# Planning fill work around pairs of Gelu blocks in a four-layer attention kernel

## The chip, the cores and the metric

The kernel runs on one core of a Trainium2 chip. The core has a matrix engine (TensorE, called PE in the profile; its weight loads are PEld), a vector engine (VectorE, DVE), a scalar engine for activation functions (ScalarE, ACT), a general engine (GpSimd, POOL) and an engine that here issues DMA transfers (SyncE, SP). Each engine runs its own instructions in order, and semaphores keep them in step. The metric is the device time of one execution in microseconds (us).

## The reference, cut to what matters

Four attention layers run one after the other on x of shape (4, 1024, 256), with a context of 77 rows, 16 heads of width 16. Only the first two layers, called L0 and L1, are touched by the change, and of them the feed-forward part of L0 above all:

```python
qkv = (_ln(x, g1, be1) @ w_qkv + b_qkv)             # L0, heads of 16
k = concat([k_self, k_ctx]); v = concat([v_self, v_ctx])
scores = einsum('bthd,bshd->bhts', q, k) * scale    # 1024 x 1101, causal
attn = softmax(where(mask, scores, -inf))
x = x + einsum('bhts,bshd->bthd', attn, v)
hdn = _ln(_ln(x, g2, be2), gf, bf) @ w1 + b1        # 256 -> 1024
hdn = gelu(hdn, approximate=False)
x = x + (hdn @ w2 + b2)                             # 1024 -> 256
# L1: rmsnorm; a linear attention over Taylor features of the context
#     plus a causal window of 64; both concatenated @ Wout, added to x
# L2: cross attention with weights and a mask, layer norm
# L3: rmsnorm, cross attention, added to x -> output
```

All of it is in 32-bit floats.

## The kernel before, in words

**Steps.** L0 and L1 are worked off in steps, one for each batch `b` (4) and each group of four heads (`quad`, 4), so 16 steps for each layer. A step computes two things side by side: the row maxima of the scores of its own unit, and the exponentials and weighted sums (weights) of the unit before it. Items of both kinds are paired (`pair_up`); in a full L0 step there are 11 maxima items (`Max0`) and 12 weight items (`Sum0`), in an L1 step four `Max1` and six of `Lin1` and `Win1`.

**Bursts and gaps.** For a pair, `step` issues two bursts of score matmuls. Each burst fills two PSUM tiles `ps` (`pair_tile`, pool `big`, two buffers, line 40): one half is for the maxima and is read by VectorE (lines 644 and 651, in L1 line 1113), the other is for the weights and is read by an Exp on ScalarE (line 716, in L1 lines 1151 and 1189). An item without a partner gets a burst in which both tiles have the same reader. Since there are two buffers and a burst takes both, the next burst's matmuls wait until ScalarE and VectorE have read this one. The time between is a gap, in which PE does other work: behind the second burst of a pair the weighted sums of the item before (matmuls pv, pvw or pvl from pe), and then fill.

**Fill.** Fill is the work of other stages that runs along: projections (pp, ppv) of the next unit, products of the context for the later layers, and the feed-forward part of an earlier batch (`ffn`, line 856). Each is a Python generator that issues one piece at each `next`, wrapped in a `Job` (line 440) with its number of pieces in this step, the share of the step over which they are to be spread (`a` to `b`) and, for work on PE, the planned time of one piece, `us`. The functions `jobs0` and `jobs1` list the jobs of each step. `gap` runs the pieces without a planned time up to the present share (layer norms, transposes, statistics, on VectorE, GpSimd and PE); `fill` runs pieces with a planned time, always of the job that is most late, until the planned time of the gap is used.

**The plan of a step.** `step` estimates for each burst how long PE must be kept busy in the gap behind it (`reads`), from the columns `c` that its readers read and the columns `f` of the sums that stand in the gap anyway. Then it raises or lowers all of them by one level until they add up to the fill work of this step (`needs`):

```python
reads = [0.3 + n * (0.1 + c / 455.0) - f / 600.0 for *_, n, c, f in bursts]
...
needs = [max(0.0, r + lo) for r in reads]
```

What a gap uses too much or too little is carried to the next (`left`; `put` counts the issued matmul columns / 600). The share of the step that is passed to `gap` and `fill` is the sum of the needs so far by their total.

**The feed-forward part.** `ffn` of one batch is 64 pieces of 0.85 planned us. The 1024 rows are cut into four blocks. For each block eight pieces compute ph (256 columns, two matmuls each), with the bias added by VectorE into a tile hT (line 874). With the eighth, ScalarE runs two Gelus in place, over two hT tiles of 128 x 1024 (line 880). So a pair of Gelus is issued with the pieces 8, 24, 40 and 56. Between them stand the pieces of the second product (po from w and hT) of the block before, of which every second one or more issues nothing. The 64 pieces are spread over four steps: 15, 11, 24 and 14 of them for the batches 0 and 1 (from the step (1, 2), by batch and quad, on), 15, 11, 22 and 16 for batch 2, and 17, 12, 17 and 18 for batch 3. So 16 steps hold ffn work, ten of L0 and six of L1.

ScalarE needs a table load (ACT_TABLE_LOAD) when it changes from Exp to Gelu and another on the way back.

Of the kernel before, what the change touches and what calls it, by code (L numbers as in the profile page):

```python
# [31 lines left out]
def tile_xattn_seq(ctx: ExitStack, tc: tile.TileContext, d: dict, out: bass.AP):  # L32
# [6 lines left out]
    work = first.enter_context(tc.tile_pool(name="work", bufs=2))  # L39
# [4 lines left out]
    put = [0.0]  # L44
# [395 lines left out]
    class Job:  # L440

        def __init__(self, gen, n, a=0.0, b=1.0, rest=False, us=0.0):
            self.gen, self.n, self.a, self.b, self.did, self.rest = gen, n, a, b, 0, rest
            self.us = us

        def late(self, share):

            want = self.n * min(1.0, max(0.0, (share - self.a) / (self.b - self.a)))  # L450
            return want - self.did
# [46 lines left out]
    def burst(parts):  # L498

        rows = [it.matmuls(p, ps) for it, p, ps in parts]  # L500
        for i in range(max(len(r) for r in rows)):
            for r in rows:
                if i < len(r):
                    for args, kw in r[i]:
                        mm(*args, skip_group_check=True, **kw)
        for it, p, ps in parts:
            it.take(p, ps)

    def pair_tile():
        return big.tile([P, 2, 512], F32, name="ps", tag="big")  # L510

    def step(items, jobs):

        bursts = []
        behind = 0
        for m, t in items:
            cols = max(i.cols for i in (m, t) if i)
            if m and t:  # L520
                for p in range(2):
                    bursts.append(((m, p), (t, 1 - p), p and t, 1, cols, p * behind))
            else:
                one = m or t
                bursts.append(((one, 0), (one, 1), t, 2, cols, behind if t else 0))
            if t:
                behind = t.cols
        work = sum(j.n * j.us for j in jobs)
        if work:
            reads = [0.3 + n * (0.1 + c / 455.0) - f / 600.0 for *_, n, c, f in bursts]  # L530

            lo, hi = -3.0, 30.0
            for _ in range(40):
                more = (lo + hi) / 2
                if sum(max(0.0, r + more) for r in reads) > work:
                    hi = more
                else:
                    lo = more
            needs = [max(0.0, r + lo) for r in reads]
        else:  # L540
            needs = [max(160.0, 140 + n * c - 0.8 * f) for *_, n, c, f in bursts]
        total, at, left = sum(needs), 0.0, 0.0
        for (*parts, t, _, _, _), need in zip(bursts, needs):
            burst([(i, p, pair_tile()) for i, p in parts])
            if t and pending:
                pending.pop(0)()
            at += need
            left += need
            was = put[0]
            gap(at / total, jobs)  # L550
            fill(at / total, jobs, was + left)
            left -= put[0] - was
            if t:
                pending.append(t.sums)
        for j in jobs:
            j.end()
# [1055 lines left out]
    def keep(key, gen):  # L1612
        if key not in live:
            live[key] = gen()
        return live[key]

    def jobs0(b, quad):

        j = []
        if quad % 2 == 0:  # L1620
            a = 0.4 if (b, quad) == (0, 0) else 0.0
            j.append(Job(keep(("h0", b, quad // 2), None), 1, a, a + 0.01, True))
        if (b, quad) in ((0, 0), (0, 2), (1, 0)):
            more_places()
        if b == 0 and quad == 0:
            j.append(Job(later_constants(), 3, 0.0, 0.4))
            j.append(Job(keep("c00", None), 1, 0.1, 0.2, us=0.85))
            j.append(Job(values0(0, 0), 4, 0.2, 0.8, us=0.85))
            j.append(Job(other_contexts(), 3, 0.0, 0.1))
            j.append(Job(feature_weights(), 3, 0.5, 1.0))  # L1630
            j.append(Job(values2(), 5, 0.3, 0.9, us=0.85))
            j.append(Job(keys2(), 4, 0.5, 0.9, us=0.5))
        if (b, quad) == (0, 1):
            j.append(Job(heads3("wk"), 8, 0.0, 1.0, us=1.03))
        if (b, quad) == (0, 2):
            j.append(Job(keys3(), 16, 0.0, 1.0, us=1.03))
        if (b, quad) == (0, 3):
            j.append(Job(heads3("wv"), 8, 0.0, 1.0, us=1.03))
        if (b, quad) in ((1, 0), (1, 1)):
            j.append(Job(keep("f3", folded3), 15 - 6 * quad, 0.0, 1.0, quad == 1, us=0.85))  # L1640
        if quad == 0 and b + 1 < NB:
            j.append(Job(stats0(b + 1), 8, 0.3 if b == 0 else 0.0, 1.0))
        if quad == 1:
            j.append(Job(values0(b, 1), 4, 0.15, 0.95, us=0.85))
            j.append(Job(keep(("h0", b, 1), lambda: heads0(b, 1, units)), 4, 0.0, 0.85, us=1.7))
            if b:
                j.append(Job(ffn_norms(b - 1), 24, 0.2, 1.0))
        if quad == 2:
            if b:
                j.append(Job(ffn_features(b - 1), 8, 0.0, 0.35))  # L1650
            if b + 1 < NB:
                j.append(Job(features0(b + 1), 8, 0.62, 1.0))
            else:
                j.append(Job(stats1(0), 8, 0.0, 0.5))
                j.append(Job(features1(0), 8, 0.62, 1.0))
        if quad == 3:
            if b + 1 < NB:
                j.append(Job(values0(b + 1, 0), 4, 0.15, 0.9, us=0.85))
                j.append(Job(context0(b + 1), 2, 0.0, 0.4, us=0.9))
                j.append(Job(keep(("h0", b + 1, 0), lambda: heads0(b + 1, 0, units)), 4, 0.15, 0.85, us=1.7))  # L1660
            else:
                j.append(Job(context1(0), 3, 0.3, 0.5))
                j.append(Job(values1(0, 0), 4, 0.4, 0.95, us=0.85))
                j.append(Job(keep(("h1", 0, 0), lambda: heads1(0, 0, units)), 4, 0.45, 0.85, us=1.7))
        for fb, n, a, last in (
            (b - 1, 15, 0.4, 0) if quad == 2 else (b - 1, 11, 0.0, 0) if quad == 3 else
            (b - 2, 24, 0.0, 0) if quad == 0 else (b - 2, 14, 0.0, 1),
        ):
            if fb >= 0:
                j.append(Job(keep(("ffn", fb), lambda: ffn(fb)), n, a, 0.97, last, us=0.85))  # L1670
        return j

    def jobs1(b, quad):
        j = []
        h = 4 * b + quad
        if h <= 1:
            j.append(Job(keep(("ffn", 2), None), (22, 16)[h], 0.0, 1.0, h == 1, us=0.85))
        if h == 1:
            j.append(Job(ffn_norms(3), 24, 0.2, 1.0))
        if h == 2:  # L1680
            j.append(Job(ffn_features(3), 8, 0.0, 0.3))
        if 2 <= h <= 5:
            j.append(Job(keep(("ffn", 3), lambda: ffn(3)), (17, 12, 17, 18)[h - 2],
                         0.35 if h == 2 else 0.0, 1.0, h == 5, us=0.85))
        if quad % 2 == 0:

            j.append(Job(keep(("h1", b, quad // 2), None), 1, 0.0, 0.01, True))
        if quad < 2:

            j.append(Job(keep(("h1", b, 1), lambda: heads1(b, 1, units)), 2,  # L1690
                         0.0 if quad else 0.2, 0.75 if quad else 0.95, us=1.7))
        if quad == 1:
            j.append(Job(values1(b, 1), 4, 0.15, 0.95, us=0.85))
        if b + 1 < NB:
            if quad == 1:
                j.append(Job(stats1(b + 1), 8, 0.0, 0.8))
            if quad == 2:
                j.append(Job(features1(b + 1), 8, *((0.35, 0.65) if h == 2 else (0.0, 0.5))))
            if quad == 3:
                j.append(Job(context1(b + 1), 3, 0.0, 0.3, us=0.85))  # L1700
                j.append(Job(values1(b + 1, 0), 4, 0.2, 0.95, us=0.85))
            if quad > 1:
                j.append(Job(keep(("h1", b + 1, 0), lambda: heads1(b + 1, 0, units)), 2,
                             0.0 if quad == 3 else 0.7 if h == 2 else 0.55, 0.75 if quad == 3 else 1.0, us=1.7))
        cb, half, n, a, last = (
            (b - 1, 0, 8, 0.0, 1), (b - 1, 1, 4, 0.4, 0), (b - 1, 1, 8, 0.0, 1), (b, 0, 4, 0.4, 0)
        )[quad]
        if cb >= 0:
            j.append(Job(keep(("comb", cb, half), lambda: combine1(cb, half)), n, a, 1.0, last, us=0.75))
        return j  # L1710
# [136 lines left out]
```

## Time and profile before

| | us |
|---|---|
| median of three runs | 2319.71 (2314.33 to 2328.15) |
| the profiled execution | 2315.78 |
| its span, first to last instruction | 2314.1 |
| TensorE busy | 2143.2 |
| VectorE busy | 1512.5 |
| ScalarE busy | 1027.2 |
| GpSimd busy | 642.6 |
| first and last Gelu pair, start of its table load | 445.0 and 1363.4 |
| one Exp over two heads (128 x 1024) | 1.024 |
| one Gelu (128 x 1024) | 1.050 |
| one table load | 1.283 |

The steps with ffn work lie between about 436 and 1400 us of the span. A line of a timeline reads: start in us, duration, engine, line, operation, tile written <- tiles read, shape, number of instructions merged; in brackets the idle time of the engine before it and what ended that. A line of groups ends with the busy time in us, the mean ns of one instruction, and the idle time before them with what ended it. A line of windows has the window, its length, the busy time of PE, PEld, DVE, ACT and POOL with the number of instructions, the granted TensorE clock (1.00 is full), the DMA share and GB/s. Matmuls overlap in the pipeline, so the durations of a merged group are a little longer than the distance to the next group.

### The profile page before, as it was taken

How to read it: one execution, taken by the hardware profiler on the slowest of the kernel's cores; microseconds unless marked ns; L12 is line 12 of the kernel's file. 1: busy time of each engine (PE TensorE's matmuls, PEld its weight loads, DVE VectorE, ACT ScalarE, POOL GpSimd, SP SyncE). 2: the span in 40 equal slices, each digit the busy share in tenths (PEclk: the TensorE clock that was granted, in tenths of full speed). 3: DMA queues.
4: the chain of work that ended last, by engine and by line, in shares of the span. 5: the costliest groups of instructions: out<-in, count | busy, mean ns of one | idle time of the engine just before them, and what ended most of it. 6: DMA issues, size and time to landing. Idle time of an engine off the chain costs nothing.

```text
span 2314.1 us, 41236 instructions
## 1 busy us (share of the span) xinstructions
PE 2143.2 (93%) x16842; PEld 1356.8 (59%) x16874; DVE 1512.5 (65%) x2492; ACT 1027.2 (44%) x1700; POOL 642.6 (28%) x927
## 2 busy tenths in 40 slices
PE   4999998999999999999989999999889998899999
PEld 2444444455555555455456666656556777788887
DVE  3756567755576545755386567777759999677664
ACT  1244444434444444344433444444448876432222
POOL 2011113011131112310152233333323655542221
PEclk9999999999999999999999999999999999999999
DMA  7221121100000000101010010101023334102200
GB/s 218 55 66 57 43 57 38 40 6 15 5 17 2 10 11 6 38 1 19 3 18 6 15 31 15 21 17 19 15 77 123 115 108 127 47 15 58 58 14 17
DMA packets 87858, 93.98 MB, mean 41 GB/s; under 512 B 35714, under 2 KB 77558, under 8 KB 87542
## 3 DMA queue, kind: packets, MB, share of 16 engines
q1 hardware_dynamic: 87670, 91.35, 15.0%
q8 instruction: 133, 2.18, 0.4%
q14 instruction: 55, 0.45, 0.1%
HBM read 55.31 MB, written 18.39 MB: 32 GB/s over the span
## 4 chain that ended last, share of the span: by engine, by line
PE 66%; DVE 16%; ACT 5%; issue 2%; POOL 1%; DMA 0%; ACTq 0%; SPq 0%; DVEq 0%; POOLq 0%
PE ps L51 27%; PE po L51 13%; PE pp L51 5%; DVE mpart L651 4%; PE ph L51 4%; PE pv L51 4%; DVE ms L1113 3%; PE psT L1350 2%; PE pvT L51 2%; PE ppv L51 2%; DVE mrow L1117 1%; PE pm L570 1%; ACT pe L716 1%; PE ptx L339 1%; PE pvw L51 1%
## 5 line engine op out<-in xcount | busy, mean ns | idle before, releaser
L51 PE MATMUL ps<-qk 32*128 32x192 f32 (+8 forms) x6528 | 589.5, 425 | 72.9 <-DVE mpart L651 32.0
L716 ACT ACTIVATE pe<-ps 128x1024 f32<-128x1024 f32 (+2 forms) x384 | 363.3, 952 | 581.5 <-PE ps L51 574.2
L51 PEld LDWEIGHTS ps<-qk 32*128 32x128 f32 (+1 forms) x6528 | 316.9, 183 | 335.4 <-DVE mpart L651 96.8
L651 DVE TENSOR_REDUCE mpart<-ps 128x2 f32<-128x1024 f32 (+4 forms) x384 | 331.1, 885 | 233.4 <-PE ps L51 232.7
L719 POOL TENSOR_SCALAR_AFFINE_SELECT pe<-pe 128x256 f32<-128x256 f32 (+1 forms) x192 | 94.9, 495 | 672.6 <-ACT pe L716 671.8
L1189 ACT ACTIVATE pew<-ps 128x768 f32<-128x768 f32 x128 | 103.4, 811 | 165.9 <-PE ps L51 165.6
L1351 ACT COPY pT<-psT 128x512 f32<-128x512 f32 (+1 forms) x192 | 92.3, 518 | 175.4 <-PE psT L1350 174.9
L1194 POOL TENSOR_SCALAR_AFFINE_SELECT pew<-pew 128x512 f32<-128x512 f32 x128 | 81.7, 638 | 302.2 <-ACT pew L1189 302.2
L51 PE MATMUL pv<-pe,va 128*32 128x512 f32 (+3 forms) x1536 | 157.1, 496 | 0.0
L1113 DVE TENSOR_TENSOR ms<-ps,maskw 128x768 f32<-128x768 f32 x128 | 122.1, 954 | 45.6 <-PE ps L51 42.7
L51 PE MATMUL po<-U,pT 128*128 128x256 f32 (+1 forms) x640 | 143.7, 380 | 0.2
L51 PE MATMUL ps<-G,xT 128*128 128x308 f32 x512 | 143.0, 423 | 0.0
L1448 ACT ACTIVATE s<-s,nm 128x77 f32<-128x77 f32 x512 | 131.2, 349 | 17.0 <-DVE nm L1489 16.9
L51 PE MATMUL ph<-yT,w 128*128 128x256 f32 x512 | 134.4, 398 | 1.2 <-DVE win L596 0.8
L644 DVE TENSOR_REDUCE mpart<-ps 128x8 f32<-128x1024 f32 x64 | 78.2, 1224 | 86.0 <-PE ps L51 83.5
L51 PEld LDWEIGHTS po<-U,pT 128*128 128x128 f32 (+1 forms) x640 | 119.2, 190 | 15.5 <-ACT pT L1351 0.6
L1588 POOL TENSOR_TENSOR s<-s,den 128x1232 f32<-128x1232 f32 x32 | 71.9, 2248 | 202.4 <-DVE den L1587 176.9
L51 PE MATMUL po<-w,hT 128*128 128x128 f32 (+1 forms) x800 | 124.6, 309 | 1.1 <-DVE lin L596 1.1
L1117 DVE TENSOR_REDUCE mrow<-ms 128x4 f32<-128x768 f32 x128 | 122.2, 955 | 4.4
L51 PEld LDWEIGHTS po<-w,hT 128*128 128x128 f32 x800 | 108.9, 191 | 23.6 <-issue 15.6
L51 PEld LDWEIGHTS ph<-yT,w 128*128 128x128 f32 x512 | 93.3, 195 | 41.5 <-issue 27.5
L51 PEld LDWEIGHTS ps<-G,xT 128*128 128x128 f32 x512 | 92.4, 190 | 26.8
(200 smaller groups left out, 3341.3 us busy)
## 6 DMA issues: line engine op xcount, KB each, us to landing
side<-in_fside_t SPq DMA_DIRECT2D x32, 616.0 KB
qk<-st SPq DMA_DIRECT2D x256, 64.0 KB
side<-in_mask_t SPq DMA_DIRECT2D x32, 154.0 KB
G<-kept_g SPq DMA_DIRECT2D x4, 1232.0 KB
U<-kept_u SPq DMA_DIRECT2D x4, 1152.0 KB
x<-in_x SPq DMA_DIRECT2D x8, 512.0 KB
out<-x SPq DMA_DIRECT2D x32, 128.0 KB
kept_g<-st SPq DMA_DIRECT2D x22, 154.0 KB
```

The source lines that it names most:

```text
L51: nc.tensor.matmul(o, lhsT, rhs, start=start, stop=stop, **kw)
L644: nc.vector.tensor_reduce(mpart[self.own][:, :, 2 * p : 2 * p + 2, 0].rearrange("p t j -> p j t"), ps.rearrange("p j (t n) -> p j t n", n= ...
L651: nc.vector.tensor_reduce(mpart[bl][:, i, 2 * p : 2 * p + 2, ci], ps[:, :, o : o + w], axis=AX.X, op=ALU.max,)
L716: nc.scalar.activation(pp[:n, :, o:512], ps[:n, :, o:512], AF.Exp, scale=SC)
L719: nc.gpsimd.affine_select(out=own, in_=own, compare_op=ALU.is_ge, fill=0.0, base=0, pattern=[[0, 2], [0, k], [1, P]], channel_multiplier=-1,)
L1113: nc.vector.tensor_tensor(v, ps.rearrange("p j (i n) -> p j i n", i=2)[:, :, :, 0:n], (maskw[:, 1:2] if w else maskw).unsqueeze(1).to_broa ...
L1117: nc.vector.tensor_reduce(mo, v, axis=AX.X, op=ALU.max, negate=True)
L1189: nc.scalar.activation(pp[:, :, :, 0 : P + WIN], ps.rearrange("p j (i n) -> p j i n", i=2)[:, :, :, 0 : P + WIN], AF.Exp, scale=SC,)
L1194: nc.gpsimd.affine_select(out=pf[:, :, 0:P], in_=pf[:, :, 0:P], compare_op=ALU.is_ge, fill=0.0, base=0, pattern=[[0, 4], [1, P]], channel_ ...
L1351: nc.scalar.copy(pT[:, 4 * group : 4 * group + n, :], ps[:, 0:n, :])
L1448: nc.scalar.activation(hs, hs, AF.Exp, bias=p1["nm"][:, h : h + 1], scale=SC)
L1588: nc.gpsimd.tensor_tensor(s3, s3, den.unsqueeze(2).to_broadcast([P, H, S]), ALU.mult)
```

## The change

`Job` gets a tuple `held`: the piece numbers, counted within this step, with which a pair of Gelus is issued. `gelus` works it out and keeps count over the steps of a batch. `step` takes 1.8 us for each such pair out of the fill work before it sets the level of `needs`. After each gap it counts the Gelu pairs that were issued in it, and adds 1.8 us for each to the need of the next gap, the one behind the following burst. The share that is passed to `gap` and `fill` counts this time with it. Everything else, all operations, tiles and transfers among it, is the same.

```diff
+        def holds(self, done):
+            return sum(1 for k in self.held if done < k <= self.did)
...
+    GELU = 1.8
+
+    ffn_done = {}
+
+    def gelus(b, n):
+
+        at = ffn_done.get(b, 0)
+        ffn_done[b] = at + n
+        return tuple(k - at for k in range(8, 64, 16) if at < k <= at + n)
...
         work = sum(j.n * j.us for j in jobs)
+        extra = GELU * sum(len(j.held) for j in jobs)
         if work:
+            work -= extra
             reads = [0.3 + n * (0.1 + c / 455.0) - f / 600.0 for *_, n, c, f in bursts]
...
-        total, at, left = sum(needs), 0.0, 0.0
+        total, at, left, held = sum(needs) + extra, 0.0, 0.0, 0
         for (*parts, t, _, _, _), need in zip(bursts, needs):
             burst([(i, p, pair_tile()) for i, p in parts])
             if t and pending:
                 pending.pop(0)()
+            need += GELU * held
             at += need
             left += need
-            was = put[0]
+            was, done = put[0], [j.did for j in jobs]
             gap(at / total, jobs)
             fill(at / total, jobs, was + left)
             left -= put[0] - was
+            held = sum(j.holds(k) for j, k in zip(jobs, done))
...
-                j.append(Job(keep(("ffn", fb), lambda: ffn(fb)), n, a, 0.97, last, us=0.85))
+                j.append(Job(keep(("ffn", fb), lambda: ffn(fb)), n, a, 0.97, last, us=0.85, held=gelus(fb, n)))
```

The three ffn jobs of `jobs1` get `held` in the same way.

## The prediction

> **What bounds the kernel now.** I read the page first, then the granted clock, then the waits of TensorE in the steps that carry feed-forward work, then single gaps on a timeline. TensorE (PE) is busy for 93% of the span and is the first entry of the chain that ended last:
>
> ```profile
> span 2314.1 us, 41236 instructions
> PE 2143.2 (93%) x16842; PEld 1356.8 (59%) x16874; DVE 1512.5 (65%) x2492; ACT 1027.2 (44%) x1700; POOL 642.6 (28%) x927
> PE 66%; DVE 16%; ACT 5%; issue 2%; POOL 1%; DMA 0%; ACTq 0%; SPq 0%; DVEq 0%; POOLq 0%
> ```
>
> So time is won only where PE stands still or runs slower. ScalarE (ACT) is far from full on average, but it has 16 short places where it is the bound. The next lines are ScalarE's groups between 440 and 1375 us:
>
> ```profile
> L880 ACT ACTIVATE hT<-hT 128x1024 f32<-128x1024 f32 x32 | 32.4, 1050 | 3.1 <-DVE hT L874 2.9
> L880 ACT ACT_TABLE_LOAD x16 | 20.5, 1283 | 0.3
> L716 ACT ACT_TABLE_LOAD x11 | 14.1, 1283 | 0.2
> ```
>
> A pair of Gelu blocks is one table load (1.28), two Gelus (2.10) and, before the next Exp, another table load (1.28): 4.7 us in which no score tile is read. The timeline of one pair, ScalarE first and then PE, shows what that does:
>
> ```profile
> 578.45 1.02 ACT L716 ACTIVATE pe<-ps 128x1024 f32<-128x1024 f32 x1 [1.30 <-PE ps L51]
> 579.49 1.28 ACT L880 ACT_TABLE_LOAD   x1
> 580.79 2.00 ACT L880 ACTIVATE hT<-hT 128x1024 f32<-128x1024 f32 x2
> 582.81 1.28 ACT L716 ACT_TABLE_LOAD   x1
> 584.10 1.02 ACT L716 ACTIVATE pe<-ps 128x1024 f32<-128x1024 f32 x1
> ```
>
> ```profile
> 578.74 1.89 PE L51 MATMUL ph<-yT,w 128*128 128x256 f32 x8
> 580.56 1.16 PE L51 MATMUL ps<-qk 32*128 32x128 f32 x20
> ...
> 582.19 1.06 PE L51 MATMUL pv<-pe,va 128*32 128x512 f32 x8
> 585.18 2.09 PE L51 MATMUL ps<-qk 32*128 32x512 f32 x8 [1.93 <-ACT pe L716]
> 587.20 2.69 PE L51 MATMUL ph<-yT,w 128*128 128x256 f32 x8
> ```
>
> The burst at 580.56 follows the Gelus; its Exp starts only at 584.10. In the gap behind it the scheduler put the sums (pv) and no fill at all, so PE idles 1.93 us for the tile. What follows is slow too: eight ph matmuls take 2.69 us where they took 1.89 before. These three windows of 4 us (all other ones from 440 to 1200 show 1.00) have the granted clock in the last but two columns:
>
> ```profile
> 533.80:537.80 4.00, 4.00 (x24) 2.33 (x26) 0.48 (x1) 1.02 (x1) 0.64 (x1) 0.57 0.00 0
> 585.00:589.00 4.00, 3.82 (x13) 2.02 (x14) 1.23 (x1) 1.15 (x2) 0.00 (x0) 0.57 0.02 4
> 861.50:865.50 4.00, 4.00 (x16) 2.57 (x16) 2.13 (x3) 1.02 (x1) 0.00 (x0) 0.57 0.00 0
> ```
>
> All three lie directly behind a Gelu pair.
>
> **What the stalls behind Gelus cost today.** For each of the 16 pairs I took the second burst behind it: the idle time in front plus what it took beyond the same burst undisturbed (1.07 us for eight matmuls of 512 columns). The second part is a stall too: the half burst for VectorE runs alone and PE then waits for the half for ScalarE. In order of time, in us: L0 steps 1.12, 1.68, 1.93, 1.23, 1.12, 1.68, 1.93, 1.23, 1.24, 1.83; L1 steps 2.50, 0, 0, 0.90, 0.92, 0. Sum 19.3. To it come the three slow stretches, (1 - 0.57) x 4.0 = 1.72 each, 5.2 together. So 24.5 us, 1.06% of the span, is all that the change can win directly.
>
> **The change, part by part.** *Added fill.* No operation is added or removed, and no DMA moves by itself; only the gap in which a piece of fill is issued. Every step that holds ffn work has exactly one Gelu pair (pieces 8, 24, 40, 56 of 64 against the shares 15, 11, 24, 14 and 22, 16, and 17, 12, 17, 18), each inside its step, not at the end. So each such step sets 1.8 us aside: one ffn piece is 512 columns / 600 = 0.85 planned and eight ph matmuls in 1.82 measured say 0.91, so about two more pieces, 1.72 us by the rate of the 0.215 us a ph matmul. They go behind the first burst after the Gelus, where PE waits now. Each stall shrinks by at most 1.72: 19.3 less the rests of 0.21 twice, 0.11 and 0.78 makes 18.0.
>
> *The slow stretches.* They go with the stalls that precede them; a rest of 0.2 us is below the 0.32 us stalls that occur every few gaps between 589 and 861.5 at a clock of 1.00. Gain 5.2.
>
> [...]
>
> *Fill taken elsewhere.* A step's fill is fixed work, so about 2.1 pieces (1.8 / 0.85) leave its other 22 gaps. In a full L0 step the planner's 23 reads add up to 25.8 us against 12.8 to 22.1 us of work: it is short everywhere. With 21.35 us of work (quad 3) a gap behind a first half falls from 1.33 to 1.25, one behind a second half from 0.48 to 0.40. The price of a lost piece is in the timeline:
>
> ```profile
> 513.56 1.52 PE L51 MATMUL ps<-qk 32*128 32x512 f32 x8
> ...
> 516.97 1.14 PE L51 MATMUL ps<-qk 32*128 32x512 f32 x8
> 518.04 1.07 PE L51 MATMUL pv<-pe,va 128*32 128x512 f32 x8
> 519.42 1.14 PE L51 MATMUL ps<-qk 32*128 32x512 f32 x8 [0.32 <-DVE mpart L651]
> ```
>
> After sums alone the next burst waits 0.32 us for VectorE's maximum; with a piece it starts 0.6 us after the tile is free and costs nothing. A first-half gap with one piece instead of two makes the burst 1.52 instead of 1.14, 0.38. Bounds for a lost piece: 0 (a gap with spare fill) and its whole length, 0.86. I take 0.35, the mean of the two rows, because most gaps hold one piece or two. Ten L0 steps: 10 x 2.1 x 0.35 = 7.4 (0 to 18.1). In the six L1 steps work exceeds the reads (22.1 against 11.8 us in the first), cover is there and I take half a piece of 0.35 a step, 1.0 in all; its bounds are 0 and 6 x 2.1 x 0.86 = 10.8.
>
> *What else moves.* Pieces without a planned time (norms, transposes) follow the same share and jump by 1.8/22 in the long gap: about two VectorE norm pieces of 0.4 to 0.9 us, beside 1.7 us of added PE work; nothing, unless that cover is gone, when the maximum behind them is late by those 2 us once a step. A moved pp piece is evicted by ScalarE, queued behind the Gelus and the Exp, and holds one of three small PSUM buffers; the piece that wants its buffer would wait as the burst does now. The spread DMAs on SyncE's queue follow the last projection piece; they move by less than one gap and serve a unit of the next step. GpSimd's selects follow the Exp and are not moved past anything. I cost these at 0; they are part of the second rival. The early pieces after the fourth pair of a batch (po, which reads the Gelu's result) can wait at most until the Gelus end, before the present wait ends.
>
> [...]
>
> *Sum.* 18.0 + 5.2 - 7.4 - 1.0 = 14.8 us won. The bounds are 23.2 won (nothing lost elsewhere) and 18.0 + 5.2 - 18.1 - 10.8 = 5.7 lost. The profiled execution took 2315.78 us (span 2314.1); the median of three is 2319.71, 3.9 higher. The sum on the median gives 2305.
>
> **The rivals.** *Half the gain is lost to what fills the gap.* Where projection pieces are the late ones (five L0 steps with heads work: 1.68, 1.23, 1.68, 1.23, 1.83), the added piece itself waits for ScalarE through its PSUM buffer, and the stall only changes its name. For it: at 1077.7 the pp piece behind the Gelus is evicted at 1083.2. Against it: three buffers, and two pieces rarely fill them. Gain lost 7.6 and one slow stretch 1.7: 14.8 - 9.3 = 5.5 won, 2314.
>
> *The starved gaps fall to half clock: slower.* If each lost piece costs its whole 0.86 and the stalls grow long enough to halve the clock, 18.0 + 5.2 - 18.1 - 1.0 = 4.1 remains, and 2.4 new slow stretches of 1.72 eat it; one in each of ten L0 steps gives 4.1 - 17.2 = 13 lost, 2333. For it: at 532.9 a stall of only 0.74 was followed by half clock. Against it: stalls of 0.32 never are.
>
> *The change does nothing*: the extra is drowned in the carry from gap to gap, which already goes over or under by a piece. 2320. Against it: the carry is at most one piece, 1.8 is two.
>
> **How the numbers follow.** Within 0.5% (11.6 us) a measurement of this kernel can't be told from no change. Chances: the sum 0.47, ending beyond that bound; half the gain 0.40 and nothing 0.03, both within it; half clock 0.10. So faster 0.47, same 0.43, slower 0.10. The likeliest alone spans 2296 (nothing lost elsewhere) to 2308. The range takes in the second and third case: 2295 to 2322, and leaves out the slower one and the ends.
>
> **What would show it.** Right: behind the Gelu pairs, two more ph or po pieces after the first burst, no wait for pe over 0.4 us, and a clock of 1.00 from 440 to 1200; some 0.32 us waits for mpart more. Wrong: waits for pe of over 1 us that remain behind Gelus (fill not placed, or spent on pieces that wait themselves), or new windows at 0.5 away from Gelus.

## The result and the profile after

The change makes the kernel slower: 2333.74 us median of five runs against 2315.36 us before, a ratio of 1.0075 (95% interval 1.0058 to 1.0093). The forecast was 2305 us, the range 2295 to 2322: 14.8 us were to be won, and 18.4 were lost. One of the ten executions of the kernel with both rules below was slow, 2490.3 us at a granted clock of 0.846, and is left out of its figures. The page of the kernel after:

```profile
span 2331.9 us, 41235 instructions
PE 2150.7 (92%) x16842; PEld 1361.5 (58%) x16874; DVE 1513.3 (65%) x2492; ACT 1027.8 (44%) x1700; POOL 641.5 (28%) x927
PE 66%; DVE 18%; ACT 4%; issue 2%; POOL 2%; DMA 0%; DVEq 0%; SPq 0%; ACTq 0%; POOLq 0%
```

The work is the same (each engine's instruction count is); the span is 17.8 us longer. In the timeline of the third Gelu pair, ScalarE first and then PE, the change did what it says:

```profile
585.02 1.28 ACT L899 ACT_TABLE_LOAD   x1
586.32 2.00 ACT L899 ACTIVATE hT<-hT 128x1024 f32<-128x1024 f32 x2
588.33 1.28 ACT L735 ACT_TABLE_LOAD   x1
589.63 1.02 ACT L735 ACTIVATE pe<-ps 128x1024 f32<-128x1024 f32 x1
```

```profile
586.46 1.14 PE L51 MATMUL ps<-qk 32*128 32x512 f32 x8
587.53 2.86 PE L51 MATMUL ph<-yT,w 128*128 128x256 f32 x12
590.31 1.52 PE L51 MATMUL ps<-qk 32*128 32x512 f32 x8
```

Three ph pieces (twelve matmuls) now stand where PE idled for 1.93 us, and the next burst loses 0.38 us only. Counted as in the prediction, the stalls of the second burst behind a Gelu pair fall from 19.7 us (19.3 in the prediction) to 2.7 in all 16 pairs. And yet the steps with ffn work take longer. To see where, I put a mark at the first score matmul of every step and took from each length half of its time at half clock (a granted clock of 0.5, read from the trace's clock record). This table is worked out from the two traces in that way:

```
                       before            after      after less before
                length at half   length at half   at full  half-clock
step              us    clock      us    clock     clock      cost
L0 (1,2)        67.01    0.0     71.06    6.8      +0.64     +3.41
L0 (1,3)        70.07    3.4     66.94    0.0      -1.43     -1.71
L0 (2,0)        70.56    3.4     69.39    0.0      +0.54     -1.71
L0 (2,1)        68.91    0.0     70.90    3.4      +0.29     +1.71
L0 (2,2)        67.11    0.0     69.97    3.4      +1.15     +1.71
L0 (2,3)        68.49    0.0     66.95    0.0      -1.54      0
L0 (3,0)        70.56    3.4     69.39    0.0      +0.53     -1.71
L0 (3,1)        68.91    0.0     69.30    0.0      +0.39      0
L0 (3,2)        68.91    0.0     72.79    6.8      +0.47     +3.41
L0 (3,3)        70.27    0.0     70.52    0.0      +0.25      0
L1 first        60.21    0.0     60.10    3.4      -1.82     +1.71
L1 second       43.95    0.0     49.99    3.4      +4.33     +1.71
L1 third        54.87    6.8     55.91   10.2      -0.67     +1.71
L1 fourth       44.95    0.0     42.72    0.0      -2.23      0
L1 fifth        43.03    0.0     43.26    0.0      +0.23      0
L1 sixth        43.90    0.0     49.91    3.4      +4.30     +1.71
sum            981.7             999.1              +5.4     +11.9
```

All other steps agree within 0.4 us. So there are two losses by this count: 5.4 us at full clock, although 17 us of stalls are gone, and 12 us of half clock.

Three groups stand out. The first are the second and the sixth L1 step. PE in the sixth, after the change:

```profile
1380.00 1.03 PE L51 MATMUL ph<-yT,w 128*128 128x256 f32 x4
1383.83 5.41 PE L51 MATMUL po<-w,hT 128*128 128x256 f32 x16 [2.81 <-ACT hT L899]
1389.17 0.93 PE L51 MATMUL ps<-qk 32*128 32x192 f32 x16
```

The ph piece at 1380.00 is number 56, which issues the Gelus. The next ffn pieces are the po that read them, and now they follow in the same gap: PE waits 2.81 us for ScalarE, and most of the po then run at half clock (the last window below). Before, the same pair was the last thing in its gap:

```profile
1363.18 1.99 PE L51 MATMUL ph<-yT,w 128*128 128x256 f32 x8
1365.11 1.10 PE L51 MATMUL ps<-qk,kf 32*77 32x512 f32 x8
1366.13 0.75 PE L51 MATMUL pvw<-pew,va 128*32 128x192 f32 x16
1366.82 0.66 PE L570 MATMUL pm<-ident,mrow 128*128 128x128 f32 x4
1367.31 3.62 PE L51 MATMUL po<-w,hT 128*128 128x256 f32 x16
```

There a burst, sums and transposes lay in between and po waited for nothing. In the second L1 step the same happens twice, 1.82 and 3.27 us; the second wait is longer because the later Gelu itself waits 4.2 us for a bias that VectorE adds behind five norm pieces.

The second group are the L0 steps with ffn features, quad 2. PE in the first of them, after the change:

```profile
415.70 1.53 PE L51 MATMUL ps<-qk 32*128 32x333 f32 x16
417.16 0.44 PE L339 MATMUL ptx<-ident,xn 128*128 128x128 f32 x2
418.54 0.33 PE L339 MATMUL ptx<-ident,xn 128*128 128x128 f32 x1 [0.94 <-DVE xn L318]
419.28 0.47 PE L339 MATMUL ptx<-ident,xn 128*128 128x128 f32 x1 [0.41 <-DVE xn L318]
419.68 2.09 PE L51 MATMUL ps<-qk 32*128 32x333 f32 x16
```

The transposes ptx now share a gap with the norm piece that makes their input xn. In this step's whole length PE idles 2.6 us for xn, against 0.9 before.

The L0 steps (2,1) and (3,1) have another such wait. VectorE first and then PE, in the first of them, after the change:

```profile
646.82 2.28 DVE L318 TENSOR_SCALAR y<-x,mv,rs 128x256 f32<-128x256 f32 x4 [2.26 <-POOL rs L293]
649.22 1.10 DVE L670 TENSOR_REDUCE mpart<-ps 128x2 f32<-128x922 f32 x1
650.37 1.55 PE L51 MATMUL ps<-qk 32*128 32x128 f32 x20 [1.51 <-DVE mpart L670]
```

Four norm pieces run ahead of the maximum for which the next burst waits, so PE idles 1.51 us, in both steps; before the change it has no such wait there.

The third is half clock. The windows shown (clock in the last but two columns) lie in steps where there was none before. Those at 418.9, 651.0, 1193.7 and 1384.9 begin during or just behind the waits named above, and that at 698.8 behind the same ptx waits in the next feature step:

```profile
418.90:425.70 6.80, 6.42 (x39) 3.43 (x40) 2.48 (x5) 1.54 (x2) 0.81 (x2) 0.50 0.00 0
651.00:654.40 3.40, 3.07 (x24) 2.81 (x19) 1.48 (x3) 1.02 (x1) 2.29 (x4) 0.50 0.03 5
698.80:702.20 3.40, 3.40 (x26) 1.21 (x20) 1.13 (x3) 1.02 (x1) 0.64 (x1) 0.50 0.00 0
1193.70:1197.10 3.40, 3.06 (x7) 2.52 (x8) 0.00 (x0) 0.29 (x1) 2.03 (x3) 0.50 0.02 5
1384.90:1388.30 3.40, 3.40 (x10) 2.68 (x9) 0.00 (x0) 0.00 (x0) 0.00 (x0) 0.50 0.35 73
```

Two more stand in L0 (3,2) and one in the first L1 step, and the third L1 step has 10.2 us instead of 6.8. The three windows behind Gelu pairs that the prediction showed are gone.

### The profile page after: what moved, and what is told of

It is laid out like the page before. It is cut to its first block, busy times and chain, and to the rows that moved or that the text cites. A ratio compares the mean times of both kernels' runs of the same rounds, so it can differ in the third digit from the quotient of the medians.

```text
span 2331.9 us, 41235 instructions
## 1 busy us (share of the span) xinstructions
PE 2150.7 (92%) x16842; PEld 1361.5 (58%) x16874; DVE 1513.3 (65%) x2492; ACT 1027.8 (44%) x1700; POOL 641.5 (28%) x927
## 4 chain that ended last, share of the span: by engine, by line
PE 66%; DVE 18%; ACT 4%; issue 2%; POOL 2%; DMA 0%; DVEq 0%; SPq 0%; ACTq 0%; POOLq 0%
PE ps L51 27%; PE po L51 13%; PE pp L51 5%; PE pv L51 5%; PE ph L51 4%; DVE mpart L670 4%; DVE ms L1132 3%; PE psT L1369 2%; DVE mrow L1136 2%; PE ppv L51 2%; PE pvT L51 1%; PE ptx L339 1%; PE pm L589 1%; ACT s L1467 1%; PE pvw L51 1%
## 5 line engine op out<-in xcount | busy, mean ns | idle before, releaser
L51 PE MATMUL ps<-qk 32*128 32x192 f32 (+9 forms) x6528 | 588.0, 428 | 69.4 <-DVE mpart L670 37.0
```

The lines of the kernel that those rows point to most:

```text
L51: nc.tensor.matmul(o, lhsT, rhs, start=start, stop=stop, **kw)
```

## The experiments

Theory A: the loss comes from what the new plan puts next to each other, po behind the Gelus that it reads, and ptx behind the norms that feed it (through the share that all jobs follow). Theory B: the fill taken out of the other gaps costs as much as the stalls give back. Theory C: half clock falls by chance. For every kernel I give the ratio to the kernel before, and for its runs the mean of span x granted clock (the time at full clock) and of the rest (lost to half clock). For the kernel before these are 2285.8 and 30.8 us in 21 runs; for the changed kernel 2293.0 and 40.1 in five. The split is rough: a straight line through the 21 runs has the span grow by 0.78 us, not 1, for each us counted as lost. So half clock is counted somewhat too high and the rest too low.

**No po in the gap of its Gelus.** An ffn job that has issued a Gelu pair rests until the next gap.

```diff
-            due = [... for i, j in enumerate(jobs) if j.us and j.did < j.n]
+            due = [... for i, j in enumerate(jobs) if j.us and j.did < j.n and not j.holds(j.was)]
...
+            for j in jobs:
+                j.was = j.did
             gap(at / total, jobs)
```

> The changed kernel with one rule more: an ffn job that has issued its Gelu pair in a gap issues nothing more in that gap, so no po stands directly behind the Gelus that it reads. Theory A (the change loses in L1's second and sixth step because po now follows the Gelus in the same gap: TensorE idles 5.1 and 2.8 us for them, and one half-clock window of 3.4 us follows in each): these two steps fall from 50.0 and 49.9 to about 44 us, the waits of po for hT vanish there, and the time is about 12 us less, 2322. Rival B (the loss comes from the fill taken out of all other gaps): po's waits vanish, but the two steps stay near 49 and the time stays within 4 us of 2334. All other steps change by under 1 us in both.

Measured: 2326.2, ratio 1.0035 (1.0023 to 1.0047). The second and sixth L1 steps fall to 46.6 and 45.9 us, without half clock there. Full clock 2290.2, lost 33.7. Two thirds of what theory A expected: the long waits for the Gelus are gone, but in the second step waits for VectorE (1.2 us of pp, 1.2 of pt, 1.5 of the bursts) take part of their place. L0 keeps its loss at full clock. That all other steps would change by under 1 us did not hold: four of them moved by 1.2 to 2.2 us, each with half clock that went or came.

**The old share for norms and transposes.** `level` is the loop that sets the needs, called once with and once without the time set aside.

```diff
+            needs, plain = level(work), level(work + extra)
...
+            even += of_plain / sum(plain)
...
-            gap(at / total, jobs)
+            gap(even, jobs)
             fill(at / total, jobs, was + left)
```

> The changed kernel, but the pieces without a planned time (norms, transposes of features, statistics) follow the share of the plan before, worked out without the Gelus; only the planned fill follows the new one. Theory A (in the three L0 steps with ffn features, quad 2 of batches 1 to 3, the shifted share puts a transposing piece into the same gap as the norm piece that feeds it; ptx waits 2.7 us for VectorE instead of 0.9, and the clock halves for 3.4 to 6.8 us): ptx waits fall back to 0.9 us a step, the three steps from 71.1, 70.0, 72.8 to about 66 to 68 us, and the time by about 12 us to 2322, while L1's second and sixth step stay near 50. Rival B (the thinned gaps): the three steps stay above 69 us and the time stays within 4 us of 2334.

Measured: 2317.1, ratio 0.9994 (0.9981 to 1.0007): nearly the whole loss is gone, 5 us more than expected. The three steps take 67.4, 67.5 and 70.2 us; the third, with one half-clock window left, is above the 66 to 68 expected. The lines of the first one that answer to those above:

```profile
414.71 2.00 PE L51 MATMUL ps<-qk 32*128 32x333 f32 x16
416.64 1.09 PE L339 MATMUL ptx<-ident,xn 128*128 128x128 f32 x8
417.79 1.24 PE L51 MATMUL ps<-qk 32*128 32x333 f32 x16
```

No ptx waits at this place, and the clock stays at 1.00 in that step. The waits of 1.51 us in (2,1) and (3,1) are gone too, which theory A had not named: at full clock these two steps gain 1.3 and 1.4 us, more than the three feature steps together (0.2, 0.8 and 0.9). The second L1 step also gains, to 46.0: its later Gelu waits 1.8 us for its bias instead of 4.2, and its half-clock window is gone; the sixth stays at 49.9, as expected. Full clock 2284.8, lost 30.3.

**Both rules together.**

> The changed kernel with both rules: no ffn piece behind its Gelu pair in the same gap, and the pieces without a planned time on the share of the plan before. Theory A (the direct stalls behind Gelus are won, 12 us net of the lost pieces, and only the two side effects lose): the effects of the two single edits add up, about 24 us less than the changed kernel, 2310, which is some 5 us under the kernel before. Rival B (thinned gaps): 2328 or more. Rival C (half clock falls by chance of where a stall lies in the 3.4 us grid, whatever the plan): the time without the half-clock windows is as in theory A, but their cost stays at 35 us or more, and the time ends between 2318 and 2328.

Measured: 2312.8 in nine runs, ratio 0.9979 (0.9965 to 0.9993). Full clock 2281.5, lost 30.6: 11.5 and 9.5 us less than the changed kernel, so the added half clock goes with the two causes, on average. The rule on po adds 3.3 us at full clock to the share's 8.2, about what it won alone (2.8).

**Taking out only.** The 1.8 us leave the other gaps and are given to none.

```diff
-            need += GELU * held
...
-        total, at, left, held = sum(needs) + extra, 0.0, 0.0, 0
+        total, at, left, held = sum(needs), 0.0, 0.0, 0
```

> One part of the change alone: the 1.8 us for each Gelu pair are taken out of the needs of all gaps, but not given to the gap behind the Gelus; what is left over is issued at the end of the step. The prediction's price of a lost piece (0.35 us for each of 21 pieces in L0, 1 us in L1) says 8 us slower than the kernel before without half-clock windows, about 2324; the stalls behind Gelus stay as before (19 us). Rival B (a lost piece costs its whole 0.86 us or more): 18 us or more slower, 2334 and above. If the share is what matters (theory A), the three L0 steps with features lose 2 to 4 us each here too, and the other seven L0 steps under 0.8 us each.

Measured: 2338.6, ratio 1.0095 (1.0077 to 1.0113), full clock 2299.9, lost 37.4. L0's ten steps are 15.6 us longer at full clock, 0.74 for each of 21 pieces: twice my price. The steps with features lose only 1.2 to 1.5 each, others up to 3.3. My price and theory A's expectation both missed here.

**Taking out only, with the old share**, asks which part of the 0.74 is the piece itself.

> What is left open: the price of a lost piece. Thinning alone cost 14.9 us at full clock in its profile (15.6 in L0, 0.74 for each of 21 pieces), the version with the old share suggests 0.39. Here the 1.8 us are taken out of the planned needs and given to no gap, but the pieces without a planned time stay on the share of the plan before. If 0.39 is the price and the rest was norms and transposes moved by the share: L0 8 us longer at full clock, the three steps with features within 1 us of before, the time about 2326. If 0.74 is the price of the pieces themselves: 14 us or more again, 2335 or more, and then the gap behind the Gelus must return more than the 11.9 us of stalls that I counted.

Measured: 2333.5, ratio 1.0083 (1.0066 to 1.0100). L0 at full clock: 10.0 us longer, 0.48 a piece; the three steps with features are within 0.25 us of before. So 5.5 of the 15.6 were norms and transposes moved by the share. The expected time is missed by 7 us: full clock 2294.3, but 38.5 lost to half clock, against 28.8 in the runs beside it. So thinned gaps, with nothing placed behind the Gelus, cost clock as well as waits. This is the part of theory B that holds.

**Time set aside in L0 only**: the jobs of L1 as before the change (one of the two lines).

```diff
-                         us=0.85, held=gelus(3, n)))
+                         us=0.85))
```

> The changed kernel with time set aside in L0's ffn jobs only; L1's steps are planned as before the change. Theory A: L1's steps return to their lengths before (43.9 for the second and sixth), which takes away 4 us at full clock and some 4 to 5 us of half clock: 2325. L0 keeps its 1 to 4 us longer steps with features. Theory B (L0's thinned gaps carry the loss): 2331 or more.

Measured: 2326.3, ratio 1.0038 (1.0025 to 1.0052), and each of L1's six steps within 0.1 us of the kernel before. L0 alone is +1.3 us at full clock in its profile, and its half clock falls into the same four L0 steps, for the same times, as in the changed kernel's. The runs' mean of 2284.1 says rather -1.7 at full clock, and 40.7 us are lost to half clock, about as much as with L1's part in. Since the split counts half clock too high, the two sources agree on this much: most of L0's loss is half clock.

**Half the time set aside**, `GELU = 0.9`.

> The changed kernel with 0.9 us set aside for a pair instead of 1.8, about one piece. Theory B (the price goes with the amount taken): about half the loss, 2325. Theory A (the price hangs on which pieces come to stand side by side): no proportion; each of the steps with features and L1's second and sixth step is either as before or at its full loss of 2 to 6 us, and the time can be anywhere from 2312 to 2335.

Measured: 2318.9, ratio 1.0000 (0.9989 to 1.0012), full clock 2283.5, lost 33.4. Not half of the loss but none at all: the three steps with features are back within 0.7 us of before, while the sixth L1 step still loses 3.4 us at full clock. That speaks for theory A, where a step has its loss or has not.

**Old share, and nothing set aside for piece 56 in L1.** The edit of the old share, and in `gelus` and `jobs1`:

```diff
+    def gelus(b, n, last=64):
...
+        return tuple(k - at for k in range(8, last, 16) if at < k <= at + n)
...
+                         us=0.85, held=gelus(3, n, 56)))
```

> The changed kernel with the pieces without a planned time on the share of the plan before, and without time set aside for the fourth Gelu pair of a batch in L1 (piece 56, behind which the next ffn pieces are the po that read the Gelus). Theory A (losses come from what the plan puts next to each other): the sixth L1 step, 49.9 us with the old share alone, is back at 44 and the second near 44 to 46, no po waits over 1 us in L1; L0 as with the old share alone. At full clock that is about 9 us under the kernel before, with the same 30 us lost to half clock: 2309. Theory B (what is taken from the other gaps costs as much as the stalls behind Gelus give back): no better than the kernel before, 2317.

Measured: 2310.4, ratio 0.9964 (0.9951 to 0.9977), faster than both kernels. Full clock 2278.6, lost 29.6; L1's second and sixth step take 43.9 us each, as before the change. PE's longest waits in the steps with ffn work, first in the changed kernel and then here:

```profile
PE ps L51 <- DVE mpart L670: 20.9, 41, 1.5
PE ptx L339 <- DVE xn L318: 9.8, 10, 1.7
PE ps L51 <- ACT pe L735: 9.2, 19, 1.2
PE po L51 <- ACT hT L899: 8.4, 5, 3.3
```

```profile
PE ps L51 <- DVE mpart L676: 19.0, 42, 1.2
PE ps L51 <- ACT pe L741: 11.0, 22, 1.2
PE ps L51 <- DVE ms L1138: 4.2, 7, 1.5
PE ptx L339 <- DVE xn L318: 3.8, 4, 1.7
```

The waits of po have left the list, and those of ptx are at the 3.8 us that they had before the change. The waits for mpart, the price of the thinned gaps, stay at 19.0 (15.9 before).

**The same with 0.9 us.**

> As the version with the old share and without L1's fourth pair, but 0.9 us set aside instead of 1.8. From the runs so far a lost piece costs 0.39 us with the old share and a placed one saves up to 0.86: in the ten L0 steps 8.5 won (of 15 us of stalls, one piece each) less 10.5 x 0.39 = 4.1, against 11.9 less 8.2 for two pieces. So within 3 us of that version at full clock. If a stall of 0.8 us is left behind most Gelus, half-clock windows can come back behind them: up to 5 us more.

Measured: 2309.0, ratio 0.9964 (0.9951 to 0.9978); full clock 2278.0, lost 29.1. One piece behind each pair wins as much as two, as the two prices say, and no more half clock came of it.

## Why the prediction was wrong, point by point

- *The stalls behind Gelus, 19.3 us, of which 18.0 won.* Right: 19.7 to 2.7, so 17.0, by the same count.
- *Fill taken elsewhere, 0.35 us a piece, 7.4 in L0.* The size was a little low. With the share held as it was: 0.48 a piece (10.0 us) when taken out alone. In the version with the old share L0 is 3.8 us shorter in its profile although its stalls fell by 12.7, which leaves 8.9, or 0.42 a piece. Taken out alone, pieces also brought half clock (37.4 and 38.5 us lost), which the sum left out; placed behind the Gelus with the old share they didn't (30.3).
- *What else moves, "I cost these at 0".* This step failed. It saw the norms and the long gap behind the Gelus, but not that lowering every other need shifts the share at which all unplanned pieces are issued, from the first gap on. In L0 the moved pieces cost 5.1 us at full clock (+1.3 against -3.8 with the old share), some of it at places up to 37 us ahead of the Gelus (417 against 454 in the first step). The case that it did name, a maximum late once a step behind norms that jump in the long gap, came in two steps at 1.51 us, and had no price in the sum either.
- *"The early pieces after the fourth pair ... can wait at most until the Gelus end, before the present wait ends."* This failed in L1. The sentence took for granted that a burst lies between the Gelu piece and po. With lower needs and long gaps, piece 56 came to stand inside a gap, with po directly behind it: 5.1 and 2.8 us of waits in two steps, which together became 8.6 us longer at full clock. L1 was given a cost of 1.0.
- *The slow stretches, 5.2 won.* The three windows did go, but new ones came at the new waits: 20.5 us lost in the steps with ffn work after, 8.5 before; over all runs 40.1 against 30.8. This term had the wrong sign, and it is the largest error: 12 of the 17.4 us in the profiled executions, or about 9 if each us counted as lost lengthens the span by 0.78 here too.
- *The rivals.* The slower one named the mechanism, half clock from new stalls, and its 2333 us is what was measured, at a chance of 0.10. The number was met by luck, since its route was another: not one window in every L0 step from starved gaps, but 6.8 us at two feature steps, 3.4 at a third and at the po waits. Neither po behind its own Gelus nor the shifted share was in any of the rivals.

At full clock, from the profiles: 17.0 won behind Gelus; lost 8.9 for thinned gaps in L0, 5.1 through the share in L0, and in L1 8.4 (4.1 net and the 4.3 of its stalls that were won). That is 5.4 lost, as in the table. The 8.9 and the 8.4 are remainders, so the sum has to close; the 10.0 us measured for thinning alone is the one independent figure beside it.

Chance has a part in the clock. With the first rule alone, the feature step (1,2) has the same two ptx waits, 0.94 and 0.41 us, as in the changed kernel, but no half clock. The windows over that step, changed kernel first:

```profile
405.20:476.20 71.00, 64.14 (x520) 35.34 (x520) 46.14 (x75) 28.64 (x31) 8.77 (x17) 0.95 0.12 33
```

```profile
407.80:476.60 68.80, 61.54 (x520) 34.06 (x520) 46.25 (x75) 28.64 (x31) 8.85 (x17) 1.00 0.12 34
```

So theory C holds for a single window. The wait of 1.51 us is another case: half clock follows it in (2,1), 0.50 from 650.99 to 654.41, and not in (3,1), where the clock is 1.00 throughout. On average, the half clock that the change adds goes with the waits of theory A and not with the thinned gaps: the versions with both causes removed have the same thinned gaps in L0 and lose 29.6 to 30.6 us, as the kernel before. What brought the window in the first L1 step stays open; PE's longest wait in the 3.4 us ahead of it is 0.49 us.

## What to carry to other kernels

A planner that serves several job lists from one running share can't be changed for one of them alone: a correction of 0.08 us a gap moved norms and transposes into the gap of the work that feeds them. Before setting time aside behind a long operation, ask which piece comes next in that queue and whether it reads the operation's result. And where the granted clock can fall, as TensorE's did here, work out the gain at full clock first: the same two waits, 0.94 and 0.41 us, were followed by 6.8 us of half clock in one execution and by none in another, so a term for it deserves a range with both signs.

## What the runs showed of the hardware that was not expected

In the profiles before and after the change, the half-clock windows of the steps with ffn work (granted clock 0.50) last 3.41 us or a multiple of it (6.83 in each, and 10.24 once, after). In each of the two they start on one grid: before the change at 534.03, 585.23, 861.71 and 1213.28, which are 15, 81 and 103 times 3.413 us apart. In the four grid intervals of 3.413 us ahead of these windows PE was busy for 78%, 44%, 44% and 57%. Other intervals of the same profile, with 53% (1134.78 to 1138.19) and 65% (1025.55 to 1028.96), were not followed by one, so in this profile busy time alone does not tell them apart.
